# A graph network with relational convolutions and attention: own PSUM banks for hot and count products, transposes in the banks of sums, a node tile finished in three places, casts issued sooner

## The chip, the cores and the metric

The kernel runs on one core of a Trainium2 chip. The core has TensorE (matrix products, in the profile PE, with PEld for its weight loads), VectorE (DVE), ScalarE (ACT), GpSimd (POOL), and SyncE (SP), which here only issues transfers. Each engine works through its own queue of instructions in order. TensorE writes its results to PSUM, which has eight banks of 128 partitions x 512 float32 values. The metric is the device time of one execution in microseconds, as a median of several runs.

## The reference

The input is a graph of 6250 nodes with 256 values each and 100000 edges, sorted by their target `dst`. The targets are distributed so that low node numbers have many edges each. Three relational layers follow one another, then a residual and a layer norm, then one attention layer with another residual and layer norm:

```
for l in range(3):                                   # W_rel: 3 x 8 x 256 x 256
    xr = einsum('nd,rde->rne', x, W_rel[l])
    msg = xr[edge_type, src]
    agg = segment_sum(msg, dst, num_segments=N)
    x = relu(agg + x @ W_root[l] + bias[l])
x = layernorm(x0 + x)
xt = (x @ weight).reshape(-1, 4, 64)
alpha = softmax(leaky_relu(einsum(xt[row], attn_l) + einsum(xt[col], attn_r)), axis=1)
tmp = einsum('nh,nhd->nd', alpha[:n], xt[col[:n]])   # the same for all heads of a node
x = layernorm(x + broadcast(tmp))
```

## The kernel before

The sums over edges are taken before the product with the weights. For every target node and each of the 8 relations, the features of the sources are added up; then one product per relation and half of the features (KC = 2) gives the node's new value.

**Steps.** In `layer`, the edges are taken in tiles of 128, four tiles to a step (GT = 4); a layer has some 163 to 179 steps, from the highest targets down, in two interleaved runs. In step i the main loop issues, in this order: background work at place 0, loads of node rows for later, the gathers of the step (`gather`, L576, one indirect transfer per tile on POOL's queue, into a pool `mp` of seven buffers), the reads of the places of the windows, the one-hot matrix for step i + 4 (`onehot`, L556), logits and `finish` of node tiles that are due, the windows (`windows`, L596), background work at place 1, some six products of the current node tile (`dense`, L663 and L667), the sums of the windows (`add`, L608), background work at place 2, and transposes of node rows (`turn`, L640).

**Windows and sums.** A window is the product of gathered features and one-hot matrix, 24 matmuls in bfloat16 for a step (three parts of each float32 value). It lands in a bank of the pool `ps_w` (four banks). VectorE adds it to the ring `S` in SBUF. With 136 columns or more a window fills a bank by itself, and the four of a step fill all four.

**Node tiles.** When all edges of a node tile are in, `fold` completes the ring, `dense` multiplies its sums by the weights into a bank of the pool `ps_d` (two banks), and `finish` adds the bias and applies the relu. For layers 0 and 1 it splits the value in three bfloat16 parts for the next layer's gathers (L697 to L704); for the last layer it adds the residual and normalises (L707 to L717). `clear` (L681) then sets the tile's part of the ring to zero on ScalarE. In the last layer, `logits` follows two steps later: a transpose (L640), ScalarE's copy of it (L643), a product with four columns (L730) and VectorE's copy (L732), one after the other. All transposes use the one bank of the pool `ps_t`.

**Background work.** The generator `jobs` hands out small pieces at the places 0, 1 and 2; the number that it yields says how many places of a step it may use. Nodes below 192 (64 in layer 0), with very many edges each, are taken out of the gathers. `starts` (L792, L797) finds where each one's edges begin, `count` fetches their edges (L839, on SP), transposes the list (L847), and counts by products with one-hot matrices (L891) how often each source and relation occurs, into `A` (L894, ScalarE); the counts go to memory as bytes (L900). `products` multiplies all nodes' features by these counts: it loads four node tiles (L935) and their counts (L938), casts both (L961, L962, L966), and takes eight matmuls into a bank (L975, a hot product), which VectorE adds to running sums (L944, L946). The products of `starts`, `count` and `products` take their banks from `ps_d` too.

The last layer needs the hot sums by step 151 (PREP_AT), when preparation of the attention begins.

Of the kernel before, what the change touches and what calls it, by code (L numbers as in the profile page):

```python
# [41 lines left out]
WB = 32  # L42
AHEAD = 4
LEAD = 6
# [129 lines left out]
def fast(tc, const, pl, x, xs, xb, src, dst, edge_type, w_rel, w_root, bias, weight,  # L174
# [10 lines left out]
    with ExitStack() as top:  # L185
# [35 lines left out]
        with ExitStack() as s:  # L221
            wp = s.enter_context(tc.tile_pool(name="wp", bufs=1))
            sp = s.enter_context(tc.tile_pool(name="sp", bufs=1))
            xp = s.enter_context(tc.tile_pool(name="xp", bufs=3))
            hp = s.enter_context(tc.tile_pool(name="hp", bufs=1))
            ps_w = s.enter_context(tc.tile_pool(name="ps_w", bufs=4, space=PSUM))
            ps_d = s.enter_context(tc.tile_pool(name="ps_d", bufs=2, space=PSUM))
            ps_t = s.enter_context(tc.tile_pool(name="ps_t", bufs=1, space=PSUM))


            mp = s.enter_context(tc.tile_pool(name="mp", bufs=7))
            op = s.enter_context(tc.tile_pool(name="op", bufs=AHEAD + 2))

            S = [sp.tile([P, KR, n * P + PAD], F32, name=f"S{f}") for f, n in enumerate(NS)]

            keep = {}
            hold = {j: sp.tile([P, D], F32, name=f"hold{j}") for j in sorted(pl.shared(pl.TM))}

            nc.vector.memset(eps, EPS)
            for t in S:  # L240
                nc.scalar.memzero(t)
            nc.sync.dma_start(bias_b, bias.rearrange("l d -> (l d)").partition_broadcast(P))
            fold_weights(tc, mp, w1x, weight, attn_l, attn_r)

            def load_w(l):

                q = nc.sync if l else nc.scalar
                wr = wp.tile([P, KC, R, D], F32, name="wr")
                wo = wp.tile([P, KC, D], F32, name="wo")
                for k in range(KC):  # L250
                    q.dma_start(
                        wr[:, k], w_rel[l, :, k * P:(k + 1) * P, :].rearrange("r p e -> p r e"))
                    q.dma_start(wo[:, k], w_root[l, k * P:(k + 1) * P, :])
                return wr, wo

            with tc.manual_schedule():
                for l in range(L):
                    wr, wo = load_w(l)
                    groups = pl.order(pl.THS[l])

                    ready = {}
                    for i, (f, g) in enumerate(groups):
                        for j in pl.reach(g):
                            ready[f, j] = i
                    if (1, 0) not in ready:
                        ready[1, 0] = ready[1, 1] - 2
                    opn = layer(
                        tc, pl, l, l == L - 1, groups, ready, S, hold, A, hd, key1, edges, cnts, flag,
                        idx, key, pos, iota, iota16, ident, wr, wo, bias_b, x, xs, xb, eps, w1x, altab, y,
                        (al3, ga, hif, yT0, lane, dst, iota_p), keep,  # L270
                        mp, op, xp, hp, ps_w, ps_d, ps_t, H)
# [250 lines left out]
def layer(tc, pl, l, final, groups, ready, S, hold, A, hd, key1, edges, cnts, flag, idx, key, pos, iota,  # L522
          iota16, ident, wr, wo, bias_b, x, xs, xb, eps, w1x, altab, y, att, keep, mp, op, xp, hp, ps_w, ps_d,
          ps_t, H):
# [111 lines left out]
    def turn(t, xT=None):  # L636

        pt = ps_t.tile([P, 4 * P], F32, name="pt")
# [45 lines left out]
    def finish(f, j, pd):  # L684
# [7 lines left out]
        nc.vector.tensor_tensor(pd[:, :D], pd[:, :D], bias_b[:, l], ALU.add)  # L692
        if not final:
# [3 lines left out]
            nc.scalar.activation(hb[:, 0], pd[:, :D], AF.Relu)  # L697
            nc.vector.scalar_tensor_tensor(rest, pd[:, :D], 0.0, hb[:, 0],
                                           op0=ALU.max, op1=ALU.subtract)
            nc.scalar.activation(h, pd[:, :D], AF.Relu)  # L700
            nc.scalar.copy(hb[:, 1], rest)
            nc.sync.dma_start(xs[l + 1][j * P:j * P + n, :], h[:n])
            nc.vector.tensor_tensor(hb[:, 2], rest, hb[:, 1], ALU.subtract)
            nc.sync.dma_start(xb[l + 1][j * P:j * P + n, :], hb[:n].rearrange("p c d -> p (c d)"))  # L704
            return
        z = xp.tile([P, D], F32, name="h", bufs=2)
# [6 lines left out]
        nc.scalar.activation(rs, mv[:, 1:2], AF.Sqrt, bias=eps)  # L713
        nc.vector.reciprocal(rs, rs)
# [3 lines left out]
        return yt  # L718

    def logits(j, yt):  # L720
# [7 lines left out]
        pt = ps_t.tile([P, 4 * P], F32, name="pt")  # L728
# [8 lines left out]
    def build():  # L737
# [22 lines left out]
        yield  # L760
        for m in range(len(blocks)):
# [7 lines left out]
            yield  # L769
# [3 lines left out]
            yield  # L773

    def starts(chunk):
# [11 lines left out]
        pc = ps_d.tile([P, 512], F32, name="pd")  # L787
        for t0 in range(LO, HI, CUT):
# [6 lines left out]
            yield  # L795
# [18 lines left out]
        yield  # L814

    def count(chunk):
# [16 lines left out]
        for a in range(nodes[0], nodes[-1], 4):  # L833
# [8 lines left out]
            yield  # L842
        ef = ei[:, G * P:2 * G * P].bitcast(F32)
        nc.vector.tensor_copy(ef, ei[:, :G * P])
        pt = ps_t.tile([P, 4 * P], F32, name="pt")
        for g in range(G):
            nc.tensor.transpose(pt[:, g * P:(g + 1) * P], ef[:, g * P:(g + 1) * P], ident)  # L847
        kk = buffer(1, F32, 4 * G * P)
# [7 lines left out]
        yield  # L856
# [15 lines left out]
        for m in range(len(pairs) + SELS - 2):  # L872
# [14 lines left out]
            if m >= SELS - 2:  # L887
                n, i, low, oh = made.pop(0)
                if i == 0:
                    pc = ps_d.tile([P, 512], F32, name="pd")  # L890
# [8 lines left out]
            yield  # L899
# [8 lines left out]
        pc = ps_d.tile([P, 512], F32, name="pd")  # L908
        nc.tensor.matmul(pc[0:1, 0:1], ones, over[:, 1:2], start=True, stop=True)
        nc.vector.tensor_tensor(flag, flag, pc[0:1, 0:1], ALU.add)  # L910
        yield

    def products():
# [34 lines left out]
        for cs in PASSES:  # L948
# [6 lines left out]
            yield  # L955
            yield
            for m, js in enumerate(loads):
# [6 lines left out]
                for u, c in enumerate(cs):  # L964
# [3 lines left out]
                    yield  # L968
                    if u == 0 and m + 1 < len(loads):
                        ts[m + 1] = load(m + 1, cs)  # L970
                    for k in range(KC):
                        ph = ps_d.tile([P, 512], F32, name="pd")
# [6 lines left out]
                        yield  # L979
                        add_up(m, held_[c][:, k], ph)  # L980
        while not {3, 4} <= set(cleared):
            yield
# [7 lines left out]
        yield  # L990
# [74 lines left out]
    def jobs():  # L1065

        if l == 0:
            for _ in build():
                yield 2
            built.append(True)  # L1070
            while step[0] < FIRST:
                yield 1
            for _ in chain(starts(0), count(0)):
                yield 3
            for _ in products():
                yield 1
            for _ in chain(starts(1), count(1)):
                yield 2
        elif l == 1:
            for _ in chain(starts(2), count(2)):  # L1080
                yield 3
            for _ in products():
                yield 1
        else:
            while step[0] < 6:
                yield 1
            for _ in products():
                yield 1
        while True:
            yield 0  # L1090

    def work(place):
        if rate[0] > place or place == 0:
            rate[0] = next(job)

    rate, step = [1], [0]
# [3 lines left out]
    if final:  # L1100
        nc.vector.memset(altab, 0.0)
    for i in range(NG + 5):
# [5 lines left out]
        step[0] = i  # L1108
        work(0)
# [5 lines left out]
        if i + AHEAD < NG:  # L1115
            ohs.append(onehot(i + AHEAD))
        for j, yt in [t for k, t in log if k <= i - 2]:
            logits(j, yt)
        log = [(k, t) for k, t in log if k > i - 2]
        for f, j, pd in fin:  # L1120
            yt = finish(f, j, pd)
            clear(f, j)
            if yt is not None:
                log.append((i, (j, yt)))
        fin.clear()
        if i < NG:
            wins = windows(i, msg, ohs.pop(0))

        work(1)
        n = PIECE * max(1, len(turned)) if i < NG else KC * (R + 1)  # L1130
        while turned and n > 0:
            if next(turned[0], False) is False:
                turned.pop(0)
                break
            n -= 1
        if i < NG:
            add(i, wins, vals)
        work(2)
        if ahead:
            next(prep, None)  # L1140
        for j in sorted(early.get(i, []), reverse=True):
            xTs[j] = turn(held.pop(j))
        for f, j in sorted((k for k, r in ready.items() if r == i), key=lambda k: -k[1]):
# [6 lines left out]
    assert not (turned or fin or log or held or xTs)  # L1150
    assert next(job) == 0 and next(prep, 0) == 0
# [546 lines left out]
```

## Time and profile before

| | |
|---|---|
| median of 9 runs | 3697.97 us (3680.97 to 3700.6) |
| the profiled execution | 3687.02 us, span 3685.1 us |
| mean granted TensorE clock | 0.866 |
| TensorE busy | 2785.1 us, 76% |
| VectorE, POOL, ScalarE busy | 1936.3, 1939.9, 845.0 us |
| gathers | 2010 transfers, 0.96 us of POOL each |
| memory traffic | 560.53 MB, mean 152 GB/s |
| first gathers of layers 0, 1, 2 | at 11.2, 1236.4 and 2395.8 us |

The profile shows one execution. Busy time of an engine counts its instructions; idle time ahead of an instruction is put down to the event that came last before it started ("issue" where the profile shows none). Engines run beside each other, so idle time matters where it lies on the engine that the rest waits for.

### The profile page before, as it was taken

Reading aid. Unit: us, or ns where it says so; the run is one execution under the profiler, and the core shown is the slowest. Engines: PE = TensorE matmul, PEld = TensorE weight load, DVE = VectorE, ACT = ScalarE, POOL = GpSimd, SP = SyncE. Lnnn points to the kernel's source line nnn. Section 1 sums busy time; section 2 is a strip of 40 time slices with the busy share of each in tenths; the row PEclk is TensorE's granted clock in tenths of the full one; section 3 lists DMA queues with packets and bytes.
Section 4 is the critical chain, followed back from the end, with each engine's and each line's share of the span. In section 5 each row is a group of like instructions: output and inputs, shape, how many; then the busy total and the mean of one; then the engine's idle time right before and its main releaser. Section 6 shows DMA issues by size and latency. Waiting matters only on the chain.

```text
span 3685.1 us, 55200 instructions
## 1 busy us (share of the span) xinstructions
PE 2785.1 (76%) x20054; PEld 2318.3 (63%) x20055; DVE 1936.3 (53%) x4564; ACT 845.0 (23%) x1178; POOL 1939.9 (53%) x2026
## 2 busy tenths in 40 slices
PE   2887878787666458888888877758888888877685
PEld 2776666666545347776766665647667676666575
DVE  6665766544445356554544444445555455544487
ACT  2321222222123123232222222202222222221114
POOL 4654555556656444555556556365444454556621
PEclk9898989988778789998988888879999898988895
DMA  4654555645545444655555555364444445445544
GB/s 138 205 169 120 148 146 144 195 138 165 144 130 151 159 115 122 199 176 157 159 163 155 176 172 157 92 190 147 136 142 137 143 140 163 147 155 145 153 146 144
DMA packets 245855, 560.53 MB, mean 152 GB/s; under 512 B 43533, under 2 KB 124452, under 8 KB 245188
## 3 DMA queue, kind: packets, MB, share of 16 engines
q0 software_dynamic: 126656, 387.18, 36.9%
q1 hardware_dynamic: 115720, 166.95, 13.3%
q8 instruction: 160, 2.62, 0.3%
q10 hardware_dynamic: 3196, 2.76, 0.2%
q14 instruction: 123, 1.01, 0.1%
HBM read 492.51 MB, written 64.21 MB: 151 GB/s over the span
## 4 chain that ended last, share of the span: by engine, by line
PE 30%; issue 8%; DVE 7%; another core or an unknown queue 6%; ACT 2%; POOL 1%; DMA 1%; DVEq 0%; POOLq 0%; ACTq 0%
PE pd L667 12%; PE pw L596 8%; PE pd L975 6%; DVE S L608 3%; PE pd L663 2%; POOL msg L576 1%; PE pt L730 1%; PE pt L640 1%; ACT u L966 1%; ACT S L681 1%; DVE oh L556 1%; DMA msg<-xb,idx 0%; ACT xT L643 0%; DVE sums L946 0%
## 5 line engine op out<-in xcount | busy, mean ns | idle before, releaser
L576 POOL DMA_INDIRECT msg<-xb,idx x1886 | 1807.5, 958 | 1513.7 <-PE pw L596 522.4
L608 DVE TENSOR_TENSOR S<-S,pw 128x320 f32 (+21 forms) x2010 | 849.1, 422 | 1027.4 <-remote 426.6
L667 PE MATMUL pd<-wr,S 128*128 128x256 f32 x4800 | 1193.8, 400 | 38.7 <-issue 23.6
L667 PEld LDWEIGHTS pd<-wr,S 128*128 128x128 f32 x4800 | 950.7, 202 | 195.4 <-issue 46.3
L596 PE MATMUL pw<-oh,msg 128*128 128x160 bf16 (+20 forms) x11316 | 830.9, 232 | 255.2 <-issue 153.1
L596 PEld LDWEIGHTS <-msg 128*128 128x128 bf16 x11316 | 734.4, 105 | 442.4 <-issue 379.7
L975 PE MATMUL pd<-u,u 128*128 128x512 f32 x1372 | 424.4, 454 | 159.5 <-DVE sums L946 47.1
L975 PEld LDWEIGHTS pd<-u,u 128*128 128x128 f32 x1372 | 281.2, 213 | 244.3 <-DVE sums L946 55.6
L643 ACT COPY xT<-pt 128x256 f32<-128x256 f32 x195 | 72.6, 372 | 1207.6 <-PE pt L640 526.0
L556 DVE TENSOR_TENSOR oh<-iota,key 128x640 bf16<-128x640 f32 (+19 forms) x475 | 320.2, 675 | 12.9 <-issue 8.0
L681 ACT ACTIVATE S<-S 128x2048 uint32<-128x2048 uint32 x150 | 286.1, 1907 | 8.5 <-DVE S L608 8.5
L663 PE MATMUL pd<-wo,xT 128*128 128x256 f32 x588 | 196.9, 461 | 51.4 <-issue 20.3
L894 ACT CAST A<-pd 128x392 uint8<-128x392 f32 x192 | 92.0, 486 | 381.2 <-PE pd L891 160.9
L966 ACT CAST u<-A 128x2048 fp32r<-128x2048 uint8 (+1 forms) x91 | 163.8, 1800 | 56.8 <-issue 44.9
L576 POOL DMA_INDIRECT msg<-in_x_dram,idx x124 | 120.9, 975 | 98.7 <-issue 31.4
L663 PEld LDWEIGHTS pd<-wo,xT 128*128 128x128 f32 x588 | 120.0, 225 | 83.2 <-issue 31.0
L891 PE MATMUL pd<-u 128*128 128x392 bf16 x284 | 93.9, 351 | 90.7 <-ACT A L894 47.0
L692 DVE TENSOR_TENSOR pd<-pd,bias_b 128x256 f32<-128x256 f32 x147 | 62.7, 426 | 175.1 <-PE pd L667 73.2
L697 ACT ACTIVATE hb<-pd 128x256 bf16<-128x256 f32 x98 | 37.7, 385 | 500.3 <-DVE pd L692 262.2
L596 PE MATMUL pw<-A,msg 128*128 128x120 f32 (+5 forms) x496 | 92.4, 345 | 40.4 <-DVE S L608 18.5
L596 PEld LDWEIGHTS pw<-A,msg 128*128 128x128 f32 x496 | 83.7, 219 | 48.2 <-DVE S L608 20.3
L962 DVE TENSOR_TENSOR u<-msg,u 128x1024 fp32r<-128x1024 f32 (+1 forms) x65 | 75.2, 1157 | 53.7 <-ACT u L961 41.0
(245 smaller groups left out, 1408.2 us busy)
## 6 DMA issues: line engine op xcount, KB each, us to landing
msg<-xb,idx POOLq DMA_INDIRECT x1886
msg<-x SPq DMA_DIRECT2D x48, 512.0 KB
xb<-hb SPq DMA_DIRECT2D x96, 192.0 KB
A<-cnts SPq DMA_DIRECT2D x72, 256.0 KB
x<-h SPq DMA_DIRECT2D x96, 128.0 KB
xin<-x SPq DMA_DIRECT2D x96, 128.0 KB
cnts<-A SPq DMA_DIRECT2D x3, 3136.0 KB
xb<-u SPq DMA_DIRECT2D x24, 384.0 KB
```

Of the source, the lines that this page charges most:

```text
L556: nc.vector.tensor_tensor(oh[:, :len(g), :w], iota[:, :w].unsqueeze(1).to_broadcast([P, len(g), w]), kk.unsqueeze(2).to_broadcast([P, len( ...
L576: nc.gpsimd.indirect_dma_start(out=msg[:, q, :], out_offset=None, in_=xb[l] if split(i) else table, in_offset=bass.IndirectOffsetOnAxis(ap ...
L596: nc.tensor.matmul(pw[:, k * w:(k + 1) * w], msg[:, q, o:o + P], oh[:, q, :w], start=(c == 0), stop=(c == parts - 1))
L608: ins = nc.vector.tensor_tensor(o, o, pw.rearrange("p (a b) -> p a b", b=W), ALU.add)
L663: nc.tensor.matmul(pd[:, :D], xT[:, k], wo[:, k], start=(k == 0), stop=False)
L667: i = nc.tensor.matmul(pd[:, :D], s[:, k * R + r], wr[:, k, r], start=(xT is None and k == r == 0), stop=(k == KC - 1 and r == R - 1))
L681: i = nc.scalar.memzero(cols(f, j))
L891: nc.tensor.matmul(pc[:, :NT * R], low, oh, start=(i == 0), stop=(i == rows_[n] - 1))
L894: nc.scalar.copy(A[:, :, c * R:(c + 1) * R], pc[:, :NT * R].rearrange("p (j r) -> p j r", r=R))
L962: nc.vector.tensor_tensor(rest[:, :g * D], t[:, :g].rearrange("p t d -> p (t d)"), top[:, :g * D], ALU.subtract)
L966: nc.scalar.copy(cn[:, :g * C], kept[m % 2][:, u * B * C:u * B * C + g * C] if l else room[:, js[0] * C:(js[-1] + 1) * C])
L975: nc.tensor.matmul(ph[:, :C], part[:, n * D + k * P:n * D + (k + 1) * P], cn[:, n * C:(n + 1) * C], start=(n == 0 and part is top), stop=( ...
```

## The change

PSUM's seven banks of the loop are divided anew: `ps_w` keeps four, `ps_d` has one, for node tiles alone, and a new pool `ps_h` of two serves `starts`, `count` and `products`. The bank of `ps_t` is gone; `turn`, `logits` and the transposes of `count` take banks of `ps_w`.

`finish` and `logits` become generators. The loop advances them at three places of a step: after the one-hot matrix, after the products of the node tile, and after the sums of the windows. For layers 0 and 1, the first part adds the bias from PSUM into SBUF and applies both relus there, the second subtracts and casts, the third stores; in the last layer the second part begins after ScalarE's square root. The clear is issued after the first part. The product of `logits` is issued in the third place of the step in which the transpose stood at the first.

Background work now says by a tuple at which places it may go on. A hot product is issued at place 0, and only if the step's estimated TensorE time is within its budget or the layer is behind its plan (`light`); its sum is issued at place 2, one product late; the casts for the next one at place 1. `count` waits four steps after its loads and one more before its transposes.

```
-            ps_d = s.enter_context(tc.tile_pool(name="ps_d", bufs=2, space=PSUM))
-            ps_t = s.enter_context(tc.tile_pool(name="ps_t", bufs=1, space=PSUM))
+            ps_d = s.enter_context(tc.tile_pool(name="ps_d", bufs=1, space=PSUM))
+            ps_h = s.enter_context(tc.tile_pool(name="ps_h", bufs=2, space=PSUM))
...
-        pt = ps_t.tile([P, 4 * P], F32, name="pt")
+        pt = ps_w.tile([P, 512], F32, name="pw")
...
-            nc.scalar.activation(hb[:, 0], pd[:, :D], AF.Relu)
-            nc.vector.scalar_tensor_tensor(rest, pd[:, :D], 0.0, hb[:, 0],
-                                           op0=ALU.max, op1=ALU.subtract)
-            nc.scalar.activation(h, pd[:, :D], AF.Relu)
+            nc.vector.tensor_tensor(h, pd[:, :D], bias_b[:, l], ALU.add)
+            nc.scalar.activation(hb[:, 0], h, AF.Relu)
+            nc.scalar.activation(h, h, AF.Relu)
+            yield
+            nc.vector.tensor_tensor(rest, h, hb[:, 0], ALU.subtract)
             nc.scalar.copy(hb[:, 1], rest)
             nc.sync.dma_start(xs[l + 1][j * P:j * P + n, :], h[:n])
+            yield
             nc.vector.tensor_tensor(hb[:, 2], rest, hb[:, 1], ALU.subtract)
...
         yT = turn(yt)
-        pt = ps_t.tile([P, 4 * P], F32, name="pt")
+        yield
+        yield
+        pt = ps_w.tile([P, 512], F32, name="pw")
...
+    def pause(k):
+        until = step[0] + k
+        while step[0] < until:
+            yield HEAD
...
-            yield
+            yield pace
+        yield from pause(4)
         ef = ei[:, G * P:2 * G * P].bitcast(F32)
         nc.vector.tensor_copy(ef, ei[:, :G * P])
-        pt = ps_t.tile([P, 4 * P], F32, name="pt")
+        yield from pause(1)
+        pt = ps_w.tile([P, 512], F32, name="pw")
...
                     for k in range(KC):
-                        ph = ps_d.tile([P, 512], F32, name="pd")
+                        if last:
+                            yield END
+                            add_up(*last)
+                        yield HEAVY
+                        ph = ps_h.tile([P, 512], F32, name="ph")
...
-                        yield
-                        add_up(m, held_[c][:, k], ph)
+                        last = m, held_[c][:, k], ph
+                        left[0] -= 1
+                    yield MID
...
+    def light(i):
+        return spent[0] < STEP * i + SLACK or left[0] > 0.9 * (last_step - i)
...
     def work(place):
-        if rate[0] > place or place == 0:
-            rate[0] = next(job)
+        if place in want[0] and (want[0] != HEAVY or light(step[0])):
+            n = left[0]
+            want[0] = next(job)
+            if left[0] < n:
+                spent[0] += HOT_US
...
+        for f, j, pd in fin:
+            closing.append(finish(f, j, pd))
+        close()
         for j, yt in [t for k, t in log if k <= i - 2]:
-            logits(j, yt)
+            closing.append(logits(j, yt))
+            next(closing[-1], None)
```

The constants are STEP 5.0, SLACK 3.0, HOT_US 1.9, DENSE_US 0.432 and TURN_US 0.45, and the places ALL (0, 1, 2), HEAD (0), HEAVY (0, 3), MID (1) and END (2); place 3 does not occur in a step, so HEAVY is place 0 under the budget.

## The prediction

> **What bounds the kernel now.** I read the engine table and the slices first (which engine, and at what clock), then TensorE's groups with the idle time ahead of each, then the waits, then equal windows, and last the timeline around single waits. The engine table and the slices:
>
> ```profile
> PE 2785.1 (76%) x20054; PEld 2318.3 (63%) x20055; DVE 1936.3 (53%) x4564; ACT 845.0 (23%) x1178; POOL 1939.9 (53%) x2026
> ...
> PEclk9898989988778789998988888879999898988895
> ```
>
> TensorE works 2785.1 of 3685.1 us and is idle 900; no other engine comes near. Where the 900 lies (name, count, busy, mean ns, then idle ahead and what ended it):
>
> ```profile
> L667 PE MATMUL pd<-wr,S 128*128 128x256 f32 x4800 | 1193.8, 400 | 38.7 <-issue 23.6 <-DVE S L649 9.5 <-DVE S L608 4.3
> L596 PE MATMUL pw<-oh,msg 128*128 128x160 bf16 (+20 forms) x11316 | 830.9, 232 | 255.2 <-issue 153.1 <-DVE S L608 62.8 <-DMA msg<-xb,idx 27.2
> L975 PE MATMUL pd<-u,u 128*128 128x512 f32 x1372 | 424.4, 454 | 159.5 <-DVE sums L946 47.1 <-issue 42.3 <-ACT u L966 22.1
> L663 PE MATMUL pd<-wo,xT 128*128 128x256 f32 x588 | 196.9, 461 | 51.4 <-issue 20.3 <-ACT h L700 19.5 <-DVE sums L946 4.6
> L891 PE MATMUL pd<-u 128*128 128x392 bf16 x284 | 93.9, 351 | 90.7 <-ACT A L894 47.0 <-issue 31.4 <-DVE most L897 3.1
> L640 PE MATMUL pt<-ident,xin 128*128 128x128 f32 x294 | 61.1, 291 | 18.7 <-ACT xT L643 15.9 <-issue 2.0 <-DVE u L851 0.5
> L730 PE MATMUL pt<-w1x,xT 128*128 128x4 f32 x192 | 34.6, 286 | 55.9 <-ACT xT L643 38.2 <-issue 17.7
> L640 PE MATMUL pt<-ident,yt 128*128 128x128 f32 x98 | 22.3, 314 | 26.7 <-ACT xT L643 13.3 <-issue 9.7 <-ACT yT L643 3.4
> L847 PE MATMUL pt<-ident,u 128*128 128x128 f32 x6 | 2.0, 434 | 58.3 <-DVE u L844 58.3
> ```
>
> The lines whose banks or place the change alters (L975, L891, L663, both L640, L730, L847) hold 461 of the 900. Not all of it is a wait that a bank can cure. The timeline shows moments when TensorE, VectorE and ScalarE stand still together:
>
> ```profile
> 2646.80 0.38 PE L640 MATMUL pt<-ident,yt 128*128 128x128 f32 x2
> 2655.43 0.37 ACT L643 COPY xT<-pt 128x256 f32<-128x256 f32 x1 [12.29 <-remote]
> 2655.85 1.01 PE L730 MATMUL pt<-w1x,xT 128*128 128x4 f32 x4 [8.67 <-ACT xT L643]
> ```
>
> The transpose is done at 2647.2, the copy needs 0.37 us, and yet it starts 8 us later. Laying the three engines' rows over each other, stretches over 0.6 us in which none works come to 307 us: 56 of L975's 159.5, 33 of L891's 90.7, 44 of the 83 of L730 and the transposes of yt and xin, 53 of L847's. I discount each line by that share, since no edit addresses such a stretch (L847's alone is a real wait: three stops for the edge list, up to 23.1 us).
>
> Gathers are the next bound. A gather takes 0.95 us of POOL and 0.30 between two, 1.25 us for a tile: 80 in 100 us. The windows shown have 50 to 66:
>
> ```profile
> 1000.00:1100.00 100.00, 64.47 (x506) 51.72 (x504) 42.12 (x115) 18.35 (x34) 56.00 (x60) 0.76 0.47 132
> 1500.00:1600.00 100.00, 90.00 (x641) 76.81 (x639) 54.68 (x104) 27.36 (x33) 53.30 (x56) 0.97 0.53 159
> 2700.00:2800.00 100.00, 85.22 (x571) 71.88 (x572) 48.87 (x106) 23.29 (x26) 47.10 (x50) 0.90 0.46 136
> 3300.00:3400.00 100.00, 72.61 (x510) 59.45 (x511) 43.97 (x107) 14.91 (x20) 62.21 (x66) 0.78 0.52 147
> ```
>
> (Columns: PE, PEld, DVE, ACT, POOL busy; clock; DMA share; GB/s.) All 2010 gathers take 2513 us, and 11 before the first, 36 and 49 at the layer changes and 143 after the last make 2752: 930 us of room.
>
> **The change, part by part**, against the profiled execution's 3687.0 us (span 3685.1); the median, 3697.97, stands 11 above.
>
> *Edge list* (L847). After the last list load the kernel goes on for 4 + 1 steps, at 6 to 7 us 30 us, before the transposes; the longest stop was 23.1. The list's 64 loads leave SP from 1263 to 1324, so some 5 us may stay. Of 58.3: **-50**. Ends 0 and -58.
>
> *Own banks for hot products* (L975). A dense tile held one of two banks, so each product waited for the sum of the one before. Releasers that go: sums, A and S 78, casts 36, together 114; less the standstill share (56/159) 74; **-70**. Ends 0 and -159.
>
> *Own banks for counts* (L891). 50 us of ACT and DVE releasers, less 33/91: **-32**. Ends 0 and -91.
>
> *Logits in two places* (L730, yt). Transpose, copy and product ran back to back; now the step's windows and dense part lie between. 82.6 less the 40 of standstill: **-45**. VectorE's 113.4 us wait on the product goes with it and lets the next finish start sooner. Ends 0 and -83.
>
> *Bank waits of L663 and of the xin transposes.* 24 and 16 by releaser, less a part: **-15**. Against it stands one dense bank instead of two: the next tile must wait for the finish's first add, which ends 0.47 us after the last matmul where VectorE is free, while the windows between (24 matmuls, 1.2 to 2.1 us) cover it. Cover gone, it costs up to 1 us for each of 147 tiles. Ends -70 and +147.
>
> *Finish in three places.* The rows "hr<-pd,hb" and "hb<-hr,hb" wait 43.6 and 46.8 us on ScalarE today; the dense part then lies between. But the 1.91 us clear now precedes ScalarE's second cast, and the window sums (L608) queue behind VectorE's subtracts. In the loop 0, ends -90 and +60; at two layer ends nothing covers it: **+4**.
>
> *Clock.* The windows go from 0.76 at 64.5 us busy to 0.97 at 90.0. The 212 us above are 5.75 in each 100, so by that slope 0.047 of clock; 2785 x (1 - 0.866/0.913) = 143 at most, 0 at least. Single rows scatter, so a third: **-45**.
>
> [...]
>
> *Transposes in the banks of sums.* 147 + 49 transposes and 48 logits products, 244 turns, now pass through the four banks that windows fill and VectorE empties. No row shows that. Above: a full wait behind a clear or a cast (1907, 1800 ns) for each, 464. Below: 0. The nearest row is "pw L596 <- DVE S L608", 81.4 us in 42 waits, on many more turns than that; and ScalarE mostly waits for the transpose (526 us in 91), not the other way round. 0.1 us each: **+25**.
>
> *Stores and counts moved.* The count of the second band, the last stage of layer 0, now ends after that layer's last gather, and its 3136 KB store stands on SP behind the last xb store and before the next weights. At 150 to 200 GB/s that is 16 to 21 us beside 2.3 MB of weights, in front of the first gathers: **+12** (0 to 25), and +3 for 12 late counts.
>
> *Pacing.* Hot products and loads keep their number; in the last layer they end 14 steps later, so early windows ease and late ones (66 gathers, 0.78 clock) fill. Hot loads share the seven gather buffers; gathers are issued some 30 us ahead of use, which hides them. Where gathers near their pitch I take back **+10** (0 to 60).
>
> Sum: 212 + 45 gained, 4 + 25 + 15 + 10 lost: 3687 - 257 + 54 = 3484, and with the median's 11, **3495**.
>
> **Rivals.**
>
> *Slower: ScalarE's copy holds a bank of sums.* If the copy of a transpose comes behind a clear or a cast, windows stand and with them all of TensorE. The gains less the other costs are 228, so it decides from 228/244 = 0.93 us a turn; at 1.9 the time is 3687 - 257 + 29 + 464 + 11 = 3934. For it: wide windows (136 columns and more) fill all four banks in each step. Against: ScalarE is 23% busy.
>
> *The second bank is worth nothing.* Standstills and late gathers already decide, and the waits of L975 and L891 reappear ahead of the windows ("issue", 153.1). Then 70, 32 and 45 fall away: 3642. [...]
>
> *All of it.* Every releaser but "issue" goes without discount, 338, and clock 80: 3687 - 338 - 80 + 54 + 11 = 3334. For it: 930 us of gather room. Against: standstills keep their trigger.
>
> **How the numbers follow.** Forecast (3400 to 3590) 0.50; second bank worthless (to 3685) 0.18; all of it 0.14; slower 0.14; within 0.3%, where 0.3% is what a measurement of this kernel can tell from nothing, 0.04. Faster 0.82. 3290 to 3680 leaves out slower, same and the tail of the best case, 0.2.
>
> **What would show it.** Idle ahead of the count transposes under 10 us; of hot products near 80; of count products near 50; of logits products near 10; waits of "pw" on ScalarE's xT copy under 30 us in all; mean clock near 0.89 to 0.9; gathers 60 and more in most windows. I am wrong if "pw" waits on ScalarE or VectorE pass 200 us, if the idle moves to "issue" ahead of L596, or if the first layer change passes 60 us.

## The result, and the profile after

The changed kernel takes 3458.06 us (median of 10 runs, 3442.0 to 3463.01), the kernel before 3698.74 in the same series (31 runs). The ratio is 0.9349, with a 95% interval of 0.9331 to 0.9366: 241 us faster. The forecast was 3495 with a range of 3290 to 3680. The time came out as forecast; several of the terms that made it did not, and the experiments show which.

The profiled execution has a span of 3465.5 us (3685.1 before). The engine table and the clock row of the page:

```profile
PE 2728.1 (79%) x20054; PEld 2284.6 (66%) x20055; DVE 1921.9 (55%) x4564; ACT 849.8 (25%) x1178; POOL 1958.3 (57%) x2026
...
PEclk8999999998787779998989898878999999998885
```

The same 20054 matmuls are busy 57 us less, at a mean granted clock of 0.881 instead of 0.866, and TensorE is idle 737 us instead of 900. Of the 220 us of span, 163 are idle time and 57 are busy time; by an estimate from the two clocks alone (2785 x (1 - 0.866/0.881)), the clock makes 47 of the 57. Line by line (name, count, busy, mean ns, then idle ahead and what ended it; L597 here is L596 before, L664 is L663, L993 is L975, L905 is L891, L736 is L730, L860 is L847):

```profile
L668 PE MATMUL pd<-wr,S 128*128 128x256 f32 x4800 | 1210.3, 403 | 35.3 <-issue 28.5 <-DVE S L609 3.2 <-DVE S L650 2.8
L597 PE MATMUL pw<-oh,msg 128*128 128x160 bf16 (+20 forms) x11316 | 824.5, 229 | 355.6 <-issue 174.9 <-DVE S L609 80.2 <-ACT xT L644 43.8
L993 PE MATMUL ph<-u,u 128*128 128x512 f32 x1372 | 395.4, 431 | 59.0 <-ACT u L981 44.0 <-issue 9.1 <-DVE rs L718 5.2
L664 PE MATMUL pd<-wo,xT 128*128 128x256 f32 x588 | 191.6, 452 | 70.4 <-DVE h L710 28.1 <-DVE h L697 20.5 <-issue 18.9
L905 PE MATMUL ph<-u 128*128 128x392 bf16 x284 | 90.5, 353 | 16.9 <-ACT A L908 13.2 <-issue 3.2 <-DVE u L897 0.4
L641 PE MATMUL pw<-ident,xin 128*128 128x128 f32 x294 | 61.9, 295 | 53.7 <-DVE S L609 27.0 <-issue 13.9 <-DMA xin<-x 7.9
L736 PE MATMUL pw<-w1x,xT 128*128 128x4 f32 x192 | 25.9, 240 | 7.4 <-ACT xT L644 7.1 <-issue 0.4
L641 PE MATMUL pw<-ident,yt 128*128 128x128 f32 x98 | 19.4, 282 | 4.0 <-DVE S L609 4.0
L860 PE MATMUL pw<-ident,u 128*128 128x128 f32 x6 | 1.3, 312 | 0.6 <-issue 0.6
```

The five lines whose own waits the change attacks (hot products, count products, logits products, transposes of yt, transposes of the edge list) fall from 391 to 88 us, by more than the whole gain. But the windows have 100 us more idle ahead of them than before (255.2 to 355.6), the transposes of xin 35 more, the wo products 19 more. So idle time moved from one line to another, and the list alone can't say which edit paid. The waits by what ended them (engine, line, what it waited for: total us, times, longest):

```profile
POOL msg L577 <- PE pw L597: 386.0, 156, 11.7
PE pw L597 <- issue: 183.3, 231, 8.1
PE pw L597 <- DVE S L609: 97.2, 51, 15.5
PE pw L597 <- ACT xT L644: 50.0, 14, 8.0
DVE altab L738 <- PE pw L736: 30.3, 16, 8.3
```

Gathers wait less for a message buffer that TensorE still reads (551.6 us before), and VectorE's wait on the logits product, 113.4 before, is down to 30.3. The windows of 100 us that the prediction showed:

```profile
1000.00:1100.00 100.00, 63.68 (x522) 50.08 (x522) 50.75 (x143) 21.86 (x43) 62.48 (x66) 0.76 0.51 145
1500.00:1600.00 100.00, 89.37 (x631) 76.24 (x631) 51.97 (x106) 25.04 (x32) 58.27 (x62) 0.90 0.53 154
2700.00:2800.00 100.00, 88.00 (x646) 76.04 (x644) 54.51 (x122) 23.29 (x26) 60.11 (x62) 0.93 0.55 162
```

62 to 66 gathers (the count in brackets behind POOL's busy time) fit in these windows where 50 to 60 did.

### The profile page after: what moved, and what is told of

The parts are those of the page before. It is cut to its first block, busy times and chain, and to the rows that moved or that the text cites. A ratio compares the mean times of both kernels' runs of the same rounds, so it can differ in the third digit from the quotient of the medians.

```text
span 3465.5 us, 55366 instructions
## 1 busy us (share of the span) xinstructions
PE 2728.1 (79%) x20054; PEld 2284.6 (66%) x20055; DVE 1921.9 (55%) x4564; ACT 849.8 (25%) x1178; POOL 1958.3 (57%) x2026
## 4 chain that ended last, share of the span: by engine, by line
PE 43%; issue 5%; DVE 5%; another core or an unknown queue 5%; ACT 2%; POOL 2%; DMA 1%; DVEq 0%; SPq 0%; POOLq 0%; ACTq 0%
PE pd L668 19%; PE pw L597 11%; PE ph L993 7%; PE pd L664 3%; POOL msg L577 2%; DVE S L609 1%; PE pw L641 1%; ACT S L682 1%; PE pw L736 1%; DMA msg<-xb,idx 1%; DVE oh L557 0%; ACT u L981 0%; PE ph L905 0%; DVE ga L1068 0%
## 5 line engine op out<-in xcount | busy, mean ns | idle before, releaser
L668 PE MATMUL pd<-wr,S 128*128 128x256 f32 x4800 | 1210.3, 403 | 35.3 <-issue 28.5
L597 PE MATMUL pw<-oh,msg 128*128 128x160 bf16 (+20 forms) x11316 | 824.5, 229 | 355.6 <-issue 174.9
L597 PEld LDWEIGHTS <-msg 128*128 128x128 bf16 x11316 | 715.1, 103 | 496.6 <-issue 427.3
L993 PE MATMUL ph<-u,u 128*128 128x512 f32 x1372 | 395.4, 431 | 59.0 <-ACT u L981 44.0
L993 PEld LDWEIGHTS ph<-u,u 128*128 128x128 f32 x1372 | 265.2, 200 | 120.2 <-ACT u L981 53.1
L644 ACT COPY xT<-pw 128x256 f32<-128x256 f32 x195 | 72.0, 371 | 906.5 <-PE pw L641 361.8
L682 ACT ACTIVATE S<-S 128x2048 uint32<-128x2048 uint32 x150 | 284.4, 1896 | 8.9 <-DVE S L609 8.9
L664 PE MATMUL pd<-wo,xT 128*128 128x256 f32 x588 | 191.6, 452 | 70.4 <-DVE h L710 28.1
L664 PEld LDWEIGHTS pd<-wo,xT 128*128 128x128 f32 x588 | 117.8, 219 | 98.3 <-DVE h L710 31.2
L698 ACT ACTIVATE hb<-h 128x256 bf16<-128x256 f32 x98 | 41.0, 418 | 562.2 <-DVE h L697 357.4
L908 ACT CAST A<-ph 128x392 uint8<-128x392 f32 x192 | 89.7, 487 | 345.3 <-PE ph L905 131.8
L597 PE MATMUL pw<-A,msg 128*128 128x120 f32 (+5 forms) x496 | 92.4, 344 | 34.4 <-DVE S L609 17.0
L597 PEld LDWEIGHTS pw<-A,msg 128*128 128x128 f32 x496 | 83.0, 218 | 42.5 <-DVE S L609 18.9
L976 ACT CAST u<-msg 128x1024 fp32r<-128x1024 f32 (+1 forms) x65 | 64.5, 992 | 182.0 <-PE ph L993 82.4
L716 ACT ACTIVATE rs<-mv,eps 128x1 f32<-128x1 f32 x49 | 14.4, 295 | 368.9 <-DVE mv L715 253.2
```

The lines of the kernel that those rows point to most:

```text
L597: nc.tensor.matmul(pw[:, k * w:(k + 1) * w], msg[:, q, o:o + P], oh[:, q, :w], start=(c == 0), stop=(c == parts - 1))
L644: nc.scalar.copy(xT.rearrange("p k n -> p (k n)"), pt[:, :D])
L664: nc.tensor.matmul(pd[:, :D], xT[:, k], wo[:, k], start=(k == 0), stop=False)
L668: i = nc.tensor.matmul(pd[:, :D], s[:, k * R + r], wr[:, k, r], start=(xT is None and k == r == 0), stop=(k == KC - 1 and r == R - 1))
L682: i = nc.scalar.memzero(cols(f, j))
L908: nc.scalar.copy(A[:, :, c * R:(c + 1) * R], pc[:, :NT * R].rearrange("p (j r) -> p j r", r=R))
```

## The experiments

The first four kernels (e1 to e4) ran on a chip on which the kernel before takes 3697 us, as above. The other eight ran on three further chips: e5 to e8 on one, e9 to e11 on another, e12 on a third. The kernel before takes 3005, 3004 and 3007 us on these, so the three are treated as one below and called the second chip; the changed kernel takes 2872 there (e9). Each ratio to the kernel before of the same series is compared with the changed kernel's ratio, 0.9555 (0.9542 to 0.9569), and 0.001 of it is 3 us.

### Banks without the order, order without the banks

First the changed kernel with the old banks (the edits of the pools are given in short, not as code):

```
-  ps_d bufs=1; ps_h bufs=2            # transposes and logits in ps_w
+  ps_d bufs=2; ps_t bufs=1            # counts and hot products in ps_d, transposes and logits in ps_t
```

> The changed kernel with the bank division of before: two banks that dense tiles, counts and hot products share, one bank for transposes and logits, four for sums. Everything else of the change (pauses, logits in two places, finish in three, pacing) stays. Theory A (banks): the idle ahead of hot and count products fell by 100 and 74 us between the two traces because of their own banks; undone, about two thirds of it returns (some 115), the banks' costs go (wo products 19, xin transposes 35, half of the 50 us of sums behind the xT copy: some 80), and the clock gives back about a third of the difference: 3458 + 35 + 12 = 3505, with hot products near 130 of idle. Theory B (order): the pauses, the two places and the pacing brought it, the banks only cost: 3400 to 3450, hot products still near 60.

Measured: 3460.74 us, ratio 0.9354 (0.9293 to 0.9414), the changed kernel's own time. Each of the 2010 window sums in this run ends within 20 us of the changed kernel's. Its lines:

```profile
L597 PE MATMUL pw<-oh,msg 128*128 128x160 bf16 (+20 forms) x11316 | 806.3, 229 | 234.5 <-issue 133.4 <-DVE S L609 54.8 <-DMA msg<-xb,idx 35.1
L993 PE MATMUL pd<-u,u 128*128 128x512 f32 x1372 | 403.7, 439 | 164.6 <-DVE sums L960 58.7 <-DVE A L960 39.2 <-ACT u L981 36.6
L664 PE MATMUL pd<-wo,xT 128*128 128x256 f32 x588 | 180.3, 431 | 25.9 <-issue 11.0 <-DVE h L710 6.5 <-DVE h L697 4.5
L905 PE MATMUL pd<-u 128*128 128x392 bf16 x284 | 92.0, 345 | 95.3 <-ACT A L908 39.9 <-issue 36.8 <-DVE most L911 8.6
L641 PE MATMUL pt<-ident,xin 128*128 128x128 f32 x294 | 59.9, 287 | 31.1 <-issue 12.5 <-DMA xin<-x 8.2 <-ACT hb L702 3.8
L641 PE MATMUL pt<-ident,xin 128*128 128x128 f32 x294 | 59.9, 287 | 31.1 <-issue 12.5 <-DMA xin<-x 8.2 <-ACT hb L702 3.8
```

The waits of hot and count products are back in full, 184 us of idle more than in the changed kernel. The windows, the wo products and the transposes of xin have 188 us less. A TensorE that is not held at the hot product is held elsewhere, mostly at the windows. Theory A falls by its time, though the idle came as it said; theory B falls by its sign (hot products still near 60), though its time is only 11 us off. Under the new order these waits cost nothing on balance: all of TensorE's idle time is 759 us here against 737, and its busy time 2702.9 against 2728.1, at a granted clock of 0.897 against 0.881. Why the clock is higher here wasn't found.

Then the old order on the new banks (the transposes of an edge list take a bank of `ps_h` here, because at their old place the windows' sums, which come later on VectorE, still hold all four banks of `ps_w`):

```
-  ps_d bufs=2; ps_t bufs=1
+  ps_d bufs=1; ps_h bufs=2            # transposes and logits in ps_w
```

> The kernel before with the new bank division alone: one bank for dense tiles, two for hot and count products, transposes and logits in the four banks of sums (the transposes of an edge list take a bank of the count products). Theory A (banks): hot and count products lose some 74 + 34 us of idle as the prediction had it, transposes cost 25 to 50, the one dense bank some 20: 3699 - 108 + 60 - 15 of clock = 3635. Theory B (order): without the new order the banks bring nothing, and back-to-back logits in the banks of sums make the windows stand behind ScalarE's copy: 3700 to 3800.

Measured: 3612.66 us, ratio 0.9764 (0.9712 to 0.9815), 22 us better than theory A; theory B falls.

```profile
L596 PE MATMUL pw<-oh,msg 128*128 128x160 bf16 (+20 forms) x11316 | 846.8, 231 | 343.1 <-issue 193.3 <-DVE S L608 68.5 <-DMA msg<-xb,idx 38.7
L975 PE MATMUL ph<-u,u 128*128 128x512 f32 x1372 | 394.6, 429 | 24.0 <-ACT u L966 16.0 <-issue 7.7 <-DVE u L962 0.2
L663 PE MATMUL pd<-wo,xT 128*128 128x256 f32 x588 | 203.5, 477 | 106.2 <-ACT h L700 58.4 <-ACT hb L697 16.3 <-DVE h L707 15.2
L891 PE MATMUL ph<-u 128*128 128x392 bf16 x284 | 89.1, 350 | 15.6 <-issue 8.6 <-ACT A L894 6.9
```

The new banks on their own are worth 85 us, the new order on its own 237, both 241. The two don't add: once the order is in, the banks add nothing that these runs can tell from zero. On the new banks and with the old finish the wo products have 106 us of idle ahead: with relus that read PSUM, the one dense bank is free only after ScalarE's second relu (58.4).

### How many banks where

> The changed kernel with one bank for hot and count products and two for dense tiles (transposes stay in the four banks of sums). Theory A: each of the 171 hot products waits for the sum of the one before and each of the 284 count products' groups for ScalarE's copy into A; 74 and 34 us return, the wo products gain 19: 3458 + 89 + 30 of clock = 3575. Theory B: the sum of a hot product is already issued at the end of a step and the next product at the start of the next, so that one bank is enough for them: 3440 to 3465, the wo products back near 50 us of idle.

```
-  ps_d bufs=1; ps_h bufs=2
+  ps_d bufs=2; ps_h bufs=1
```

Measured: 3530.58 us, ratio 0.9565 (0.9505 to 0.9626), some 70 us slower than the changed kernel. The wo products' idle falls to 9.6, and the hot products stand:

```profile
L993 PE MATMUL ph<-u,u 128*128 128x512 f32 x1372 | 422.2, 455 | 233.7 <-DVE sums L960 104.7 <-DVE A L960 59.3 <-issue 29.8
```

That lies between the two theories, nearer to A. One bank alone for hot and count products is too few; two shared with dense tiles (e1, 3460.74 us) are enough. The transposes also stand in other banks in e1; the next kernel removes that difference.

> As the kernel with one bank for hot and count products, but the bank that is free goes to transposes and logits instead of a second dense tile. Against that kernel it tells what the transposes cost in the banks of sums. If they cost what the trace after shows (idle ahead of xin transposes up by 35 us, sums behind the xT copy 50 us, some of it only moved), this one is faster than that by 40 to 70 us, less the 19 of the dense bank. If the idle in these rows is only where TensorE stands when it has run ahead (VectorE sums late), it is equal to it within 15 us, or slower by the 19.

```
-  ps_d bufs=1; ps_h bufs=2            # transposes and logits in ps_w
+  ps_d bufs=1; ps_h bufs=1; ps_t bufs=1   # transposes and logits in ps_t
```

Measured: 3557.92 us, ratio 0.9607 (0.9554 to 0.9661). It is not faster than e3, by the medians 27 us slower, with overlapping intervals. So the transposes in the banks of sums cost no more than a second dense bank is worth. That worth was not measured on this chip; if it is near the 24 us that e11 shows on the second, the cost is not the 40 to 70 us that their rows suggested.

This kernel and e1 make the cleanest pair on banks: the new order in both, four banks for sums, one for transposes, and two for dense tiles, counts and hot products. Shared among the users (e1) the two give 3460.74 us, divided into one and one (e4) 3557.92.

> The changed kernel with its three banks in one pool: dense tiles, counts and hot products take whichever of the three is free (transposes stay in the four banks of sums). If the 70 us of idle ahead of the wo products (one dense bank) lie on the path, the dense tile gets its second bank back outside the hot passes: 0.5 to 1% faster than the changed kernel of the same call. If that idle only sits there, as e1's did, equal to it within 0.3%.

```
-  ps_d bufs=1; ps_h bufs=2
+  ps_d bufs=3; ps_h = ps_d
```

Measured on the second chip: 2848.82 us, ratio 0.9487 (0.9474 to 0.9500), against 0.9555 for the changed kernel beside it: 24 us better, the fastest version here and within the 0.5 to 1% of its first theory. The wo products, first in the changed kernel and then in this one, on that chip:

```profile
L664 PE MATMUL pd<-wo,xT 128*128 128x256 f32 x588 | 168.2, 411 | 24.9 <-DVE h L710 18.3 <-DVE h L697 6.4
```

```profile
L664 PE MATMUL pd<-wo,xT 128*128 128x256 f32 x588 | 165.9, 407 | 2.2 <-ACT A L908 2.2
```

From the last gather to the end it takes 125.9 us instead of 140.2, so 14 of the 24 lie there, where the last node tiles follow one another with no windows between. This idle was on the path. The version was not run on the first chip; there, the stretch after the last gather is 157.4 us in the changed kernel and 156.8 in e4, with one bank for dense tiles, and 140.1 in e1 and 142.5 in e3, with two.

### The parts of the order, one undone at a time

These ran on the second chip. What was expected of e5 to e8 was written in times of the first; only the differences and ratios carry over. The changed kernel itself:

> The changed kernel itself, unedited, beside the kernel before. The runs e5 to e8 were made on a chip on which the kernel before takes 3005 us at a clock of 0.931 instead of 3697 at 0.867, and there the changed kernel has no time yet. If this lands there: theory A (the four undone parts each cost something) gives less than e5's 2879, near 2860, ratio 0.952; if the pauses are worth nothing there it is equal to e5, 2879, ratio 0.958. If it lands on the first chip it repeats 0.935.

Measured: 2872.45 us, ratio 0.9555 (0.9542 to 0.9569): the gain there is 4.5% instead of 6.5%. The time lies between the two that were named, 0.952 and 0.958.

> The changed kernel with the pauses of 4 and 1 steps between the last load of an edge list and its transposes taken out (transposes again at the next place after the load). By the sum's term the three stops ahead of the count transposes come back, 58 us of idle in the trace before: 3458 + 50 = 3508. Rival: as with the banks, TensorE's idle only sits there and would otherwise sit ahead of windows; then 3458 to 3475.

```
-        yield from pause(4)
+        yield END
         ...
-        yield from pause(1)
```

Measured: 2879.43 us, ratio 0.9582 (0.9564 to 0.9600), 8 us, at the edge of what the intervals tell apart: they overlap, and the two profiled executions lie 2 us apart. In its trace the transposes of the edge list have 27.8 us of idle ahead again (none in the changed kernel), but it is made good: the run is 11 us behind at the 166th of 2010 window sums, 3 us behind at the 1000th and level with the changed kernel from about the 1160th on. Counting also begins five steps sooner without the pauses; that this is what makes it good is likely and not shown.

> The changed kernel with transposes, copy and logits product of a node tile issued together again ahead of the windows. By the sum's term 45 us come back: about 3503, with the idle ahead of the logits product near 50 to 80 again. Rival: the wait comes back, but the windows behind it then find their banks free, and the time stays within 15 us of 3458.

```
         yT = turn(yt)
-        yield
-        yield
```

Measured: 2893.95 us, ratio 0.9643 (0.9621 to 0.9665), 26 us, between the term (45) and the rival (under 15). The 48 logits wait again for ScalarE's copy, 0.8 us each, and the loss arises in the last layer alone:

```profile
L734 PE MATMUL pw<-w1x,xT 128*128 128x4 f32 x192 | 29.6, 260 | 40.4 <-ACT xT L644 40.4
```

> The changed kernel with the finish of a node tile in one place ahead of the windows (add, two casts, two subtracts, both stores; in the last layer also the root and the scaling). The sum's term was 0 in the loop and 4 in favour of one place at the layer ends: 3450 to 3465. Rival: VectorE stands behind ScalarE's casts (44 + 47 us before) while four banks of sums wait to be emptied, so that the windows are late: 3500 to 3550. Which of the two holds shows in VectorE's waits on the casts and in the waits of the windows on the sums.

```
             nc.scalar.activation(h, h, AF.Relu)
-            yield
             ...
             nc.sync.dma_start(xs[l + 1][j * P:j * P + n, :], h[:n])
-            yield
             ...
         nc.scalar.activation(rs, mv[:, 1:2], AF.Sqrt, bias=eps)
-        yield
```

Measured: 2895.93 us, ratio 0.9638 (0.9622 to 0.9655), 25 us, between the term and the rival. Some 16 us are lost by the 332nd of 2010 window sums, in the first half of layer 0 while lists are counted, and little in the rest.

> The changed kernel with the hot passes in the order of before (cast, one step, load, product, one step, sum, next product; no pacing), on the new banks. The edge list of the third chunk counted has no pause here, worth at most its 23 us. The sum gave the own banks 70 us and the moved casts and the pacing nothing or a loss of 10: then 3450 to 3480. Rival: since the new order on the old banks ran in 3461, the order of the hot pass must be a large part of the gain: 3520 to 3600.

```
-            yield from pause(3)
-            yield MID
-            last = None
+            yield HEAD
+            yield HEAD
             ...
-                        if last:
-                            yield END
-                            add_up(*last)
-                        yield HEAVY
             ...
-                        last = m, held_[c][:, k], ph
-                        left[0] -= 1
-                    yield MID
+                        yield HEAD
+                        add_up(m, held_[c][:, k], ph)
```

Measured: 2918.80 us, ratio 0.9715 (0.9700 to 0.9730), 48 us: the largest of the four parts. Here the pauses of one edge list, in layer 0, are out as well; the run is level with the changed kernel at the end of layer 0, after that list, so the loss arises later and isn't theirs. The idle ahead of hot products barely differs, first in the changed kernel and then here, so this loss isn't a wait of these products:

```profile
L993 PE MATMUL ph<-u,u 128*128 128x512 f32 x1372 | 383.2, 421 | 36.6 <-ACT u L981 36.3 <-DVE u L977 0.2
```

```profile
L989 PE MATMUL ph<-u,u 128*128 128x512 f32 x1372 | 380.6, 419 | 41.0 <-ACT u L980 40.8 <-DVE u L976 0.2
```

> The kernel of e8 (hot passes in the order of before, no pacing) with the banks of before as well. The old banks cost nothing under the new order (e1: 3461 against 3458), the old order costs some 1.4% on the new banks (e8 against e5). Theory A (place and bank stand in for each other: a sum issued at the end of the step frees the shared bank as early as a bank of its own would): with both taken away the product waits for the sum again; idle ahead of hot products over 150 us, and the time is at least 2% over e8's ratio, that is 0.99 of before or more. Theory B (they are independent and the banks are worth nothing): equal to e8, ratio 0.97.

The edit is that of e8 and that of e1 together. Measured: 2918.97 us, ratio 0.9719 (0.9706 to 0.9733), equal to e8. Theory A of that run falls (the idle ahead of hot products is 57.6 us and not over 150): with pauses, logits and finish in their new places, the old banks cost nothing even under the old hot order. (In the loops this run is up to 21 us behind e8, and it wins that back after the last gather, 126.6 against 143.4 us, with two banks for dense tiles.)

> The changed kernel without the pacing of hot products: each next product goes at the start of the next step, whatever the step holds, so a chunk of a load takes two steps, against three in the order of before. The early casts and the early sums stay. The old order cost 1.6% of before's time (e8 0.9715 against e9 0.9555, same chip), 64 us of it in the first two thirds of the last layer, of which 22 came back by its end. Theory A (casts and sums issued sooner are what the new order is worth): within 0.3% of the changed kernel, 0.9555 on that chip (0.935 on the first). Theory B (the pacing is worth it, by spreading hot products over the steps of the last layer): at least half of the loss returns, 0.963 or more (0.943 on the first chip), with the last layer's first two thirds late again.

```
     def light(i):
-        return spent[0] < STEP * i + SLACK or left[0] > 0.9 * (last_step - i)
+        return True
```

Measured: 2980.73 us, ratio 0.9916 (0.9901 to 0.9930). Without the pacing, 108 of the 133 us that the whole change gains on that chip are gone. Theory A falls; but the time is also 60 us behind e8, the old order without pacing, which neither theory allowed for. Of the 108 us between the two profiled executions, TensorE's idle time takes 80 and its busy time 28 (granted clock 0.930 against 0.943). Some 53 us are lost by the end of layer 1, the rest in the last layer, where the windows of 100 us show how. The changed kernel (columns as above: PE, PEld, DVE, ACT, POOL with its gathers, clock, DMA share, GB/s):

```profile
2050.00:2150.00 100.00, 95.17 (x750) 85.12 (x748) 65.96 (x148) 23.09 (x28) 68.24 (x73) 1.00 0.61 178
2250.00:2350.00 100.00, 98.02 (x773) 85.10 (x772) 64.27 (x145) 28.65 (x30) 67.40 (x71) 1.00 0.62 190
2550.00:2650.00 100.00, 93.92 (x803) 80.13 (x803) 69.01 (x161) 30.43 (x34) 74.14 (x76) 0.98 0.66 204
```

Without pacing:

```profile
2050.00:2150.00 100.00, 98.79 (x699) 86.11 (x698) 63.00 (x131) 32.42 (x34) 52.04 (x55) 1.00 0.56 171
2550.00:2650.00 100.00, 87.08 (x790) 77.18 (x789) 62.66 (x155) 16.44 (x23) 75.71 (x80) 0.93 0.64 182
2650.00:2750.00 100.00, 77.10 (x697) 67.19 (x696) 54.59 (x140) 14.01 (x20) 75.84 (x80) 0.86 0.62 176
```

While hot products come with every step, TensorE is full (98.79) and gathers fall to 55 in 100 us; when they are used up, gathers run at their pitch, 80, and TensorE has only 77 us of work. The same work passes two limits one after the other. Spread out, both engines stay near their limit at once (98.02 and 71). The waits say the same, the changed kernel's first:

```profile
POOL msg L577 <- PE pw L597: 129.1, 119, 8.4
PE pw L597 <- DMA msg<-xb,idx: 121.9, 51, 14.6
```

```profile
PE pw L597 <- DMA msg<-xb,idx: 204.6, 97, 14.9
POOL msg L577 <- PE pw L597: 188.4, 159, 8.4
```

Both directions grow, TensorE waiting for messages and gathers waiting for TensorE. The old hot order, with three steps for each chunk of a load where the unpaced one has two, stands between in time (0.9715). So the 108 us are the price of the new hot order without its pacing; against the old hot order, the new one with its pacing gains 48.

## Why the prediction was right, and where it was not

**The sum.** It had 158 us of idle and 45 of clock; the profile has 163 and 57. Most signs that were to show it came as named: idle ahead of the edge list's transposes 0.6 us, of hot products 59 (near 80), of logits products 7.4, gathers over 60, the first layer change 40 us. Three did not: idle ahead of count products 16.9 (near 50), the wait for the xT copy 50 (under 30), the clock 0.881 (0.89 to 0.9). Of the signs of being wrong, one was passed by a little: over all products and transposes into "pw", waits on VectorE and ScalarE come to 204 us (154 ahead of the windows alone), where 200 was the bound. "Issue" ahead of the windows grew from 153.1 to 174.9 us. The parts behind the idle were wrong in both directions and cancelled; that the sum came so close is in part luck.

**Edge list, -50.** The idle went from 58.3 to 0.6 as said. Its price was not the idle: undone, it puts 27.8 us of idle back on the second chip and costs at most about 8. On the first chip it wasn't run alone.

**Own banks for hot and count products, -70 and -32.** This is the step that failed as an argument. The idle fell by 100 and 74 us, more than forecast, but e1 gives all of it back at no loss of time. The step took a line's idle, less a share for standstills, as the line's price; it didn't ask what TensorE would wait for next. As a set and in the old order the bank terms were well sized: -70, -32, -15 and +25 make -92, e2 measured -85. The rival "second bank worth nothing" names what holds under the new order, and priced it wrongly, since the same time was to be had without the banks. It holds for the banks of their own and not for a second bank as such: with one bank for hot and count products instead of two, e3 is at 0.9565 against 0.9349; e1 is no test of a single bank, as these products have two banks there too, shared. What in the new order makes own banks needless wasn't found: in e10 the hot sums are back in their old place, and the old banks cost nothing there either, on the second chip.

The discount for standstills (stretches in which TensorE, VectorE and ScalarE all stand) had a premise that failed too, that no edit addresses them. In the changed kernel 6 us of the 56 ahead of hot products are left and 1 of the 33 ahead of count products; with the old banks (e1) 41 and 29 are back. Ahead of the windows they grew from 100 to 149 us: they moved with the idle.

**Logits in two places, -45.** Right mechanism; idle of these two lines 82.6 to 11.4 us, and 26 us when undone on the second chip. (The 83 of the prediction are these two lines; of its 44 us of standstill 9 lie ahead of xin, which is not among them.)

**Bank waits of L663 and xin, -15.** Wrong sign. The two lines' idle grew from 70 to 124 us, and e11 shows that one bank for dense tiles costs 24 us on the second chip. The prediction named the cover, the windows between two tiles; at the end of the last layer there are none, and that stretch holds 14 of the 24.

**Finish in three places, 0.** Too low: 25 us on the second chip, most of it in layer 0's counting. The prediction had ends of -90 and +60 there; the time went to the first side.

**Transposes in the banks of sums, +25.** The forecast that windows wait under 30 us for the xT copy failed, 50 us in 14 waits; that is 0.2 us for each of 244 turns, far from the 0.93 at which the slower rival decides. e4 shows no gain from moving them out at the price of a dense bank; their cost by itself was not measured.

**Stores and late counts, layer ends, +12, +3 and +4.** Between the last gather of a layer and the first of the next lie 40 and 57 us (37 and 50 before), and 157 after the last gather of all (143): 24 instead of 19. The 14 after the last gather are about what e11 (14) and e1 (17) save there with more banks for dense tiles; no run tells stores and late counts apart.

**Pacing, +10.** Wrong sign, and the largest error where it could be tested. It was looked at for what it does to buffers and not for what it balances, though the prediction had the two limits, TensorE's windows at 90 of 100 us and the gathers' pitch of 80. The term was measured from the kernel before, so e8 is its test: on the second chip the new hot order, early casts and pacing together, is worth 48 us. The 108 of e12 are counted from the new order without pacing and not from the kernel before. On the first chip the order as a whole brought 237 us; its parts weren't run there, so how those 237 divide stays open. The gathers' waits for TensorE's buffers point the same way: 551.6 us before, 504.2 with the new banks alone, 377.9 with the new order alone.

**Clock, -45.** 57 us less busy at 0.881; by the prediction's own formula that clock makes 47 of them. So the term fits, and the sign beside it, 0.89 to 0.9, did not fit the term: it would have made 75 to 105 us.

## What to carry to other kernels

Idle time ahead of a line says where an engine stops, and not what an edit of that line is worth: before adding such waits up, ask what the engine would meet next, and undo one part to see whether the time follows. Where one engine runs background work beside a stream that another engine feeds at a fixed pitch, spread that work so that neither is ever alone at its limit; here the same order of work without the spreading was 108 us slower. A pool of banks shared by all users beat a fixed division among them, in e11 against e9 (0.9487 against 0.9555) and in e1 against e4 (3460.74 against 3557.92 us).

## What was not expected of the hardware

The same kernel takes 3697 us on one chip and 3005 on others (changed: 3458 and 2872), and the granted clock, 0.867 and 0.931 for the kernel before, explains only part of it. In the changed kernel's two traces (granted clock 0.881 and 0.943) TensorE is busy 2728.1 and 2507.4 us, 221 of the 595 us between the spans; the other 374 are its idle time. Instructions of the other engines last the same: a gather 967 and 966 ns, a window sum on VectorE 422 and 422, a clear 1896 and 1896. What differs beside TensorE's own products is the time between. On the first chip:

```profile
PEld L597 <- issue: 427.3, 522, 16.3
DVE S L609 <- remote: 367.9, 172, 10.9
```

On the second:

```profile
DVE S L609 <- PE pw L597: 266.5, 184, 9.4
PEld L597 <- issue: 72.2, 188, 4.1
```

There the wait on "remote", an event that the profile can't place, is not among VectorE's waits for the sums at all, and the stretches over 0.6 us in which TensorE, VectorE and ScalarE all stand add up to 51 us instead of 202. So the standstills by which the prediction discounted its lines were largely a matter of that chip. They also depend on the kernel: on the first chip they come to 307 us in the kernel before (53 of them the wait for the edge list), 241 in e2, 223 in e1 and 202 in the changed kernel. What causes them wasn't found.
